# Counts for the first half of the nodes made during the deal; bucket rows stored by rounds

## The chip, the cores and the metric

The kernel runs on one core of one Trainium2 chip. The metric is device time in microseconds (us). The core has five engines that work side by side, each through its own list of instructions in order: TensorE (PE, matrix products into PSUM), VectorE (DVE), ScalarE (ACT), GpSimd (POOL, which here mostly issues indirect DMAs and a few additions), and SyncE (SP, which issues most of the other DMAs). They meet only through semaphores.

## The reference

The reference takes 3125 nodes with 256 features, 53,125 directed edges (`src`, `dst`) sorted by `dst`, and 16 attributes an edge. It runs four residual layers. The first is a message-passing layer over the edges, the third sums neighbours twice (SAGE), the second and fourth are mixtures without edges:

```python
x = x + gnn0(layernorm(x), edge_index, edge_attr)   # h = relu([x_src, x_dst, attr] @ mW1 + mb1); messages = h @ mW2 + mb2
                                                    # summed by src; then a two-layer update, residual
x = x + ffn0(layernorm(x))                          # shared MLP + 2 of 4 experts by a gate
x = x + gnn1(layernorm(x), edge_index)              # agg = segment_sum(x[src], tgt) / max(deg, 1); two such layers
x = x + ffn1(layernorm(x))                          # router keeps the top tokens, gelu MLP, scaled
```

For the third layer the kernel does not gather along edges. It multiplies by a **table of counts**, `adj_h`: for each pair of nodes, how many edges lead from the one to the other, as 16-bit floats. The table is in two halves, `half0` for targets below `H0` = 1152 and `half1` for the rest. Filling `half0` is what the change is about.

## The kernel before

**The deal** (`deal`). The edges stand in 416 columns of 128 edges, taken as 104 chunks of four columns. A *bucket* is a block of 32 source nodes; there are 98. For each chunk, `buckets` makes one-hots of the bucket numbers (VectorE), `select` turns them into ranks within the bucket by four products on PE, `place` (VectorE) works out the row of each edge in the DRAM buffer `cbuf`, and builds the record `rt` (68 floats, 272 bytes: a one-hot of the source within its bucket, the attributes in two halves, three fields on the target), and `put` sends the four columns with four indirect scatters from GpSimd (L438). `rt` has 20 buffers, so VectorE may run up to 20 chunks ahead of GpSimd. A bucket holds up to `ROUNDS` = 5 rounds of 128 edges by rank; since the edges come sorted by target, low ranks have low targets: round 0 has only targets below `H0`, round 1 both kinds, rounds 2 to 4 only the others. This is checked with the data at the end, and the result, `fits`, chooses between the branch described here and a general one.

Beside the dealing, three times a chunk (`piece`), a generator `tables` is advanced. It normalises the nodes and writes the first layer's products by node to `tab_a`, `tab_b`, `tab_h`, `own` over SP. At the start, unused places of `cbuf` are cleared over ScalarE's DMA queue. The order on PE, VectorE, ScalarE and SP is the order of the program, written out by hand; only GpSimd's is planned by the framework.

In `cbuf` the rows are laid out by group of four buckets: within a group, partition by partition, 20 rows of 272 bytes (5 rounds times 4 buckets) together.

**The edge stage** (`edges_by_bucket`). 25 groups of four buckets (the last has two, and is taken first), five rounds each: 125 steps. `begin` loads a group's rows (`rows<-cbuf`, L790) and its nodes' products (L795) over SP. A step runs: `fetch` gathers four times 128 rows of `tab_b` by target (POOL, L807), `turned` transposes (PE L826, copies `oT`), `spread` (PE L840, `pa`), the sum and the relu (DVE L845, ACT L850), `by_source` (PE L856). The loop places the next step's `spread` ahead of this step's `by_source`. Small parts of the layers that follow are put between (`pieces`), one pair of groups behind.

Between them also runs a generator `counts`, four advances a step, for the group before: `one_hots` makes for each round and bucket one-hots of the target (`oa`, 128 wide, L881; `ob`, 288 or 512 wide, L885), PE multiplies them (`pn`, L900), ScalarE copies the sum to 16 bits (`cn`, five buffers, L107), SP writes it to `adj_h` (L905, L909). A full group has per bucket a `half0` part (rounds 0 and 1, 288 wide) and a `half1` part (rounds 1 to 4, 512 wide):

```python
return (0,) * (r * P < BOTH1) + (1,) * (r * P >= BOTH0) if u["nb"] == 4 else (0, 1)   # halves(u, r)
for i, (hf, w) in enumerate(((half0, W0), (half1, W1))):                              # in counts(u)
```

`bank(...)` takes the next of a ring of PSUM banks, eight in the deal and three in the edge stage: an allocation waits until the third one before it has been read.

**The rest.** `sums_of_few` reads `adj_h` and does both neighbour sums (L1402), then the last layer. Neither is touched.

The change touches `deal` (clears, `ends`, `place`, `put`, the loop, the checks) and `edges_by_bucket` (`begin`, `halves`, `one_hots`, `counts`, and the index of a row in `rows`).

Of the kernel before, what the change touches and what calls it, by code (L numbers as in the profile page):

```python
# [8 lines left out]
F32 = mybir.dt.float32  # L9
# [7 lines left out]
P = 128  # L17
# [6 lines left out]
GB = 4  # L24
# [22 lines left out]
BOTH0, BOTH1 = P, 2 * P  # L47


@with_exitstack  # L50
def gnn_ffn_kernel(ctx: ExitStack, tc: tile.TileContext, a: dict, out: bass.AP):
# [130 lines left out]
    def deal():  # L182
# [11 lines left out]
        def clear(g, n):  # L194
            to = bass.AP(tensor=cbuf.tensor, offset=cbuf.offset + (g * P * PER + SURE * GB) * RW,
                         ap=[[PER * RW, P], [P * PER * RW, n], [1, (ROUNDS - SURE) * GB * RW]])
            nc.scalar.dma_start(to, empty.unsqueeze(1).to_broadcast([P, n, empty.shape[1]]))

        rest_of_last = bass.AP(tensor=cbuf.tensor, offset=cbuf.offset + full * P * PER * RW, ap=[[PER * RW, P], [1, SURE * GB * RW]])
        clear(full, 1)  # L200
        half_empty = (ROUNDS - SURE) * GB
        for o in range(0, SURE * GB, half_empty):
            n = min(half_empty, SURE * GB - o) * RW
            nc.scalar.dma_start(bass.AP(tensor=cbuf.tensor, offset=rest_of_last.offset + o * RW, ap=[[PER * RW, P], [1, n]]),
                                empty[:, :n])
        for g in range(0, full, 6):
            clear(g, min(6, full - g))
# [42 lines left out]
        nc.gpsimd.iota(past, pattern=[[P, ET]], base=GROUPS_OF * P * PER, channel_multiplier=1,  # L250
# [28 lines left out]
        def ends():  # L279
            nc.vector.tensor_copy(d_f, dst)  # L280
            nc.vector.scalar_tensor_tensor(base, b_i, float(CAP), past, op0=OP.mult, op1=OP.subtract)
            nc.vector.tensor_scalar(b_i, b_i, GB - 1, None, op0=OP.bitwise_and)
            nc.vector.scalar_tensor_tensor(base, b_i, float(1 - CAP), base, op0=OP.mult, op1=OP.add)
            nc.vector.tensor_scalar(b_i, src, BN - 1, None, op0=OP.bitwise_and)
            nc.vector.tensor_copy(scr, b_i)
            nc.vector.tensor_scalar(row[:, :, AT_SRC - BN], scr, 1.0, None, op0=OP.add)

            nc.vector.tensor_scalar(hi, d_f, float(W0), None, op0=OP.is_ge)
            for j in range(2, 8):
                at = float(W0 * j - (W0 - W1) * max(j - 4, 0))  # L290
                nc.vector.scalar_tensor_tensor(hi, d_f, at, hi, op0=OP.is_ge, op1=OP.add)
            nc.vector.scalar_tensor_tensor(scr, scr, 4.0, hi, op0=OP.mult, op1=OP.add)
            nc.vector.tensor_scalar(over, d_f, float(H0), float(P - 4), op0=OP.is_ge, op1=OP.mult)
            nc.vector.scalar_tensor_tensor(row[:, :, AT_SRC + 1 - BN], over, 1.0, scr, op0=OP.add, op1=OP.add)
            nc.vector.tensor_scalar(over, hi, -4.0, 0.0, op0=OP.add, op1=OP.max)
            nc.vector.scalar_tensor_tensor(over, over, float(W0 - W1), d_f, op0=OP.mult, op1=OP.add)
            nc.vector.scalar_tensor_tensor(over, hi, -float(W0), over, op0=OP.mult, op1=OP.add)
            nc.vector.tensor_scalar(row[:, :, AT_SRC + 2 - BN], over, 1.0, None, op0=OP.add)

        bad = pl.tile([P, 4], F32, name="bad")  # L300
# [80 lines left out]
        with tc.tile_pool(name="deal", bufs=3) as dp:  # L381
# [29 lines left out]
            def place(c, out):  # L411
# [11 lines left out]
                nc.vector.scalar_tensor_tensor(f, rnd, float(GB - P * PER), base[:, at], op0=OP.mult, op1=OP.add)  # L423
                nc.vector.scalar_tensor_tensor(f, rank, float(PER), f, op0=OP.mult, op1=OP.add)
                nc.vector.scalar_tensor_tensor(f, rank, float(CAP), f, op0=OP.is_lt, op1=OP.mult)
                nc.vector.tensor_tensor(to, f, past[:, at], op=OP.add)
                pos[c] = to
                rt = dp.tile([P, GB, RW], F32, name="rt", bufs=20)
# [5 lines left out]
            def put(c):  # L434
                rt, to = rts.pop(c), pos.pop(c)
                for i in range(GB):
                    n = min(P, E - (c * GB + i) * P)
                    one_of = nc.gpsimd.indirect_dma_start(  # L438
                        out=cbuf[:], out_offset=bass.IndirectOffsetOnAxis(ap=to[:n, i:i + 1], axis=0),
                        in_=rt[:n, i, :], in_offset=None)  # L440
                    tc.declare_no_dep(one_of.ins, group="deal", reason="no two have one place")
                    tc.add_to_no_dep_group("deal", one_of.ins)

            making = tables()
            totals[-1] = dp.tile([1, NBK], F16, name="none", bufs=1)
# [3 lines left out]
            def piece(c):  # L449
                if c > 0:  # L450
                    next(making, None)

# [50 lines left out]
            nc.vector.scalar_tensor_tensor(wrong, wrong, 1.0, whole, op0=OP.mult, op1=OP.mult, accum_out=bad[:, 2:3])  # L503
            rest = dp.tile([P, 1], F32, name="rest", bufs=1)
# [3 lines left out]
            nc.vector.tensor_scalar(fits, pf[:1, :1], 0.5, None, op0=OP.is_lt)  # L508

# [6 lines left out]
    def rest_of(fast):  # L516
# [259 lines left out]
        def edges_by_bucket():  # L776
            with tc.tile_pool(name="bk", bufs=2) as bp, tc.tile_pool(name="upd", bufs=2) as up, \
# [8 lines left out]
                def begin(g):  # L786
# [3 lines left out]
                    nc.sync.dma_start(rows.bitcast(F32).rearrange("p r w -> p (r w)"),  # L790
                                      cbuf[g * P * PER:(g + 1) * P * PER, :].rearrange("(p r) w -> p (r w)", p=P))
# [4 lines left out]
                    return dict(g=g, nb=nb, m=nb * BN, ag=ag, rows=rows, oa={}, ob={})  # L796

# [4 lines left out]
                def fetch(u, r):  # L802

                    cb = bp.tile([P, 4, HID], F32, name="cb", bufs=4)
                    for j in range(u["nb"]):
                        i = GB * r + j
# [4 lines left out]
                def halves(u, r):  # L811

                    return (0,) * (r * P < BOTH1) + (1,) * (r * P >= BOTH0) if u["nb"] == 4 else (0, 1)
# [7 lines left out]
                def turned(u, r):  # L821
# [3 lines left out]
                    for j in range(nb):  # L825
                        nc.tensor.matmul(pt[:2 * BN, j * P:(j + 1) * P], lhsT=u["rows"][:, GB * r + j, :2 * BN], rhs=ident_r,  # L826
# [25 lines left out]
                def by_source(u, r, hs):  # L852
                    if r == 0:
                        u["ph"] = pH.tile([P, HID], F32, name="ph")
                    for j in range(u["nb"]):
                        nc.tensor.matmul(u["ph"][j * BN:(j + 1) * BN, :], lhsT=u["rows"][:, GB * r + j, :BN].bitcast(F32),  # L856
# [16 lines left out]
                def one_hots(u, j, rs):  # L873


                    for r in rs:
                        field = u["rows"][:, GB * r + j, AT_SRC + 1:AT_SRC + 3].bitcast(F32)
# [4 lines left out]
                        w = W0 if halves(u, r) == (0,) else W1  # L882
                        ob = bp.tile([P, W1], F16, name="ob", bufs=12)
                        u["ob"][j, r] = ob
                        nc.vector.tensor_scalar(ob[:, :w], ids[:, 1:w + 1], field[:, 1:2], None, op0=OP.is_equal)  # L885

                def counts(u):
                    made, cut = None, ROUNDS // 2
                    for part in (range(cut), range(cut, ROUNDS)):
                        one_hots(u, 0, part)  # L890
                        yield
                    for j in range(u["nb"]):
                        for i, (hf, w) in enumerate(((half0, W0), (half1, W1))):
                            if j + 1 < u["nb"]:
                                one_hots(u, j + 1, range(cut, ROUNDS) if i else range(cut))
                                yield
                            pn = bank("pn")
                            rs = [r for r in range(ROUNDS) if (j, r, i) in u["oa"]]
# [8 lines left out]
                            made = hf[b * BN:(b + 1) * BN, :].rearrange("s (h l) -> (s h) l", l=w), cn[:, :w]  # L907
                            yield
# [599 lines left out]
```

## Time and profile before

| | us |
|---|---|
| time, median of 3 runs | 2128.87 (2125.72 to 2130.82) |
| the profiled execution's own time | 2130.54 |
| its span in the trace | 2128.7 |

| stretch of the span (us) | PE busy | DVE busy | ACT busy | POOL busy | clock of PE | DMA share |
|---|---|---|---|---|---|---|
| 0 to 33, loads and first chunks | 9.4 | 26.5 | 6.2 | 2.7 | 1.00 | 0.87 |
| 33 to 500, deal | 292.4 | 391.5 | 114.1 | 349.3 | 0.74 | 0.34 |
| 500 to 581, deal, last scatters | 0.2 | 0.9 | 0.0 | 61.4 | 0.50 | 0.08 |
| 581 to 625, edge stage starts | 20.0 | 15.7 | 16.8 | 22.5 | 0.66 | 1.02 |
| 625 to 1514, edge stage | 784.6 | 669.1 | 596.6 | 500.4 | 0.95 | 0.70 |
| 1514 to 1942, neighbour sums | 400.7 | 261.7 | 153.8 | 29.0 | 0.96 | 0.45 |
| 1942 to 2129, last layer | 177.1 | 113.3 | 50.9 | 19.0 | 0.98 | 0.05 |

How to read it. A row of a group of instructions gives line, engine, operation, `out<-in` by the program's names, shapes, the count, the busy time and the mean of one in ns, and behind the second bar the idle time before them with what ended it. Busy times of PE overlap, since products are pipelined; the distance from start to start says more. A line with `[1.03 <-DVE xn L127]` says that the engine had stood idle for 1.03 us until VectorE's instruction of line 127 let it go. "Landing" of a DMA is the time from its issue to its last data.

### The profile page before, as it was taken

The page shows a single profiled execution, that of the slowest core. Times are in us where ns is not written, and L with a number is a line of the kernel's source. Part 1 is how long each engine was busy: PE and PEld are TensorE (multiplying, and loading weights), DVE is VectorE, ACT ScalarE, POOL GpSimd, SP SyncE. Part 2 cuts the span into 40 slices and gives each one's busy share as a digit, 9 for nine tenths or more (in the row PEclk, how much of TensorE's full clock was granted, in tenths as well). Part 3 has the DMA queues.
Part 4 walks back from the last instruction along what each step waited for, and adds up shares of the span by engine and source line. Part 5 has one row for each costly group of instructions (what it writes and reads, how often), then busy time and mean ns, then how long its engine had stood idle before and what let it go on. Part 6 is the DMA issues. An engine that isn't in the chain of part 4 may idle for free. (4 is left out here: it accounts for less than half of the span.)

```text
span 2128.7 us, 25119 instructions
## 1 busy us (share of the span) xinstructions
PE 1684.2 (79%) x7419; PEld 1025.3 (48%) x7419; DVE 1478.7 (69%) x4078; ACT 938.4 (44%) x1695; POOL 984.3 (46%) x1044
## 2 busy tenths in 40 slices
PE   3667676661068898898889889888859999999998
PEld 1333232320034554455455546555537777886666
DVE  6888888883048877786777777677436675667960
ACT  1222222220046776676666666667333333443222
POOL 3677777777657655655565565555000000111011
PEclk9777777775579999999999999999979999999999
DMA  9432332320199776777667667774234545550010
GB/s 297 113 107 97 106 115 87 126 97 31 41 302 279 211 226 207 212 207 218 201 208 216 202 202 215 209 220 129 73 114 125 135 116 145 140 152 1 1 40 23
DMA packets 238441, 316.46 MB, mean 149 GB/s; under 512 B 34458, under 2 KB 168968, under 8 KB 237928
## 3 DMA queue, kind: packets, MB, share of 16 engines
q1 hardware_dynamic: 182216, 164.43, 25.6%
q0 software_dynamic: 52512, 142.96, 23.0%
q10 hardware_dynamic: 3568, 7.38, 1.0%
q8 instruction: 61, 1.00, 0.2%
q14 instruction: 84, 0.69, 0.1%
HBM read 229.71 MB, written 84.96 MB: 148 GB/s over the span
## 5 line engine op out<-in xcount | busy, mean ns | idle before, releaser
L807 POOL DMA_INDIRECT cb<-tab_b,goes_to x490 | 473.4, 966 | 372.4 <-issue 108.6
L438 POOL DMA_INDIRECT cbuf<-rt,to x416 | 410.4, 986 | 166.6 <-issue 98.6
L845 DVE TENSOR_TENSOR cb<-pa,cb 128x1024 f32<-128x1024 f32 x245 | 288.8, 1218 | 97.8 <-PE pa L840 57.4
L1402 PE MATMUL padj<-z,slab 128*128 128x512 f32 x1250 | 323.0, 411 | 15.3 <-DVE z L1311 15.3
L850 ACT ACTIVATE cb<-cb 128x1024 f32<-128x1024 f32 x245 | 254.9, 1051 | 58.0 <-DVE cb L845 57.1
L1402 PEld LDWEIGHTS padj<-z,slab 128*128 128x128 f32 x1250 | 233.6, 192 | 75.0 <-issue 23.0
L107 ACT ACTIVATE oT<-pt 64x512 fp32r<-64x512 f32 (+1 forms) x250 | 144.9, 580 | 176.7 <-PE pt L826 173.7
L900 PE MATMUL pn<-ob,oa 128*128 128x512 f16 (+1 forms) x596 | 153.4, 368 | 50.9 <-ACT cn L107 36.2
L130 POOL TENSOR_TENSOR x<-x,xn 128x256 f32<-128x256 f32 x25 | 24.6, 983 | 354.9 <-DVE xn L127 354.9
L840 PE MATMUL pa<-gives,oT 128*128 128x512 f32 x490 | 165.8, 460 | 22.7 <-ACT oT L107 10.4
L885 DVE TENSOR_SCALAR ob<-ids,rows 128x512 f16<-128x512 f16 (+1 forms) x490 | 171.9, 351 | 0.0
L881 DVE TENSOR_SCALAR oa<-ids,rows 128x128 f16<-128x128 f16 x596 | 150.3, 268 | 0.0
L343 PE MATMUL pp<-mw,xTa 128*128 128x512 f32 x200 | 137.7, 843 | 10.3 <-ACT xTa L107 10.3
L107 ACT ACTIVATE cn<-pn 128x288 f16<-128x288 f32 x196 | 97.2, 496 | 103.9 <-PE pn L900 90.4
L856 PE MATMUL ph<-cb,rows 128*32 128x512 f32 x980 | 140.9, 617 | 1.3 <-ACT cb L850 1.1
L900 PEld LDWEIGHTS <-oa 128*128 128x128 f16 x596 | 53.3, 100 | 162.9 <-issue 98.7
L331 PE MATMUL pt<-ident,xn 128*128 128x128 f32 x50 | 16.7, 438 | 134.8 <-DVE xn L326 134.8
L840 PEld LDWEIGHTS pa<-gives,oT 128*128 128x128 f32 x490 | 93.9, 204 | 54.3 <-ACT oT L107 15.0
L826 PE MATMUL pt<-ident_r,rows 128*64 128x128 f32 x490 | 52.8, 232 | 84.8 <-DMA rows<-cbuf 84.8
L1329 ACT ACTIVATE slab<-two 128x2048 fp32r<-128x2048 f16 x50 | 95.6, 1912 | 40.2 <-PE padj L1402 39.6
L107 ACT ACTIVATE total<-pk 1x98 f16<-1x98 f32 x103 | 24.5, 238 | 178.4 <-PE pk L404 178.3
L826 PEld LDWEIGHTS pt<-ident_r,rows 128*64 128x64 f32 x490 | 50.6, 143 | 106.3 <-issue 87.7
(242 smaller groups left out, 3040.0 us busy)
## 6 DMA issues: line engine op xcount, KB each, us to landing
two<-adj_h SPq DMA_DIRECT2D x24, 1600.0 KB, 7.7
rows<-cbuf SPq DMA_DIRECT2D x25, 680.0 KB, 9.2
adj_h<-cn SPq DMA_DIRECT2D x100, 128.0 KB, 3.1
gives<-tab_h SPq DMA_DIRECT2D x48, 256.0 KB, 10.8
cb<-tab_b,goes_to POOLq DMA_INDIRECT x490, 4.4
adj_h<-cn SPq DMA_DIRECT2D x100, 72.0 KB, 3.3
cbuf<-rt,to POOLq DMA_INDIRECT x416, 2.2
cbuf<-empty ACTq DMA_DIRECT2D x4, 1632.0 KB
```

Of the source, the lines that this page charges most:

```text
L107: nc.scalar.activation(dst, src, AF.Copy)
L343: nc.tensor.matmul(pp, lhsT=xT[:, c, :], rhs=mw1[:, 2 * h + c, :], start=c == 0, stop=c == 1)
L438: one_of = nc.gpsimd.indirect_dma_start(out=cbuf[:], out_offset=bass.IndirectOffsetOnAxis(ap=to[:n, i:i + 1], axis=0), in_=rt[:n, i, :], i ...
L807: nc.gpsimd.indirect_dma_start(out=cb[:, j, :], out_offset=None, in_=tab_b[:], in_offset=bass.IndirectOffsetOnAxis(ap=u["to"][:, i:i + 1], ...
L840: nc.tensor.matmul(got[j // 2][:, j % 2, :], lhsT=oT[:, j, :], rhs=u["ag"][:, j, :], start=True, stop=True)
L845: nc.vector.tensor_tensor(cb[:, j:j + 2], pa, cb[:, j:j + 2], op=OP.add)
L850: nc.scalar.activation(h, h, AF.Relu)
L856: nc.tensor.matmul(u["ph"][j * BN:(j + 1) * BN, :], lhsT=u["rows"][:, GB * r + j, :BN].bitcast(F32), rhs=hs[j // 2][:, j % 2, :], start=r ...
L881: nc.vector.tensor_scalar(oa, ids[:, 1 + i * P:1 + (i + 1) * P], field[:, 0:1], None, op0=OP.is_equal)
L885: nc.vector.tensor_scalar(ob[:, :w], ids[:, 1:w + 1], field[:, 1:2], None, op0=OP.is_equal)
L900: nc.tensor.matmul(pn[:, :w], lhsT=u["oa"].pop((j, r, i)), rhs=u["ob"][j, r][:, :w], start=r == rs[0], stop=r == rs[-1])
L1402: nc.tensor.matmul(pa, lhsT=slab[:, c, :], rhs=(z2 if second else z1)[:, c, :], start=c == 0, stop=c == NB - 1)
```

## The change

Rows in `cbuf` are laid out by rounds: all groups' rows of one round stand together, the rounds in falling order, the spare rows (for edges that have no place) first. `STRIDE` is one round of all groups. Scatters from chunk `LATE` = 70 on are declared to reach only the part `cbuf[:PLACED]`, which leaves out rounds 0 and 1 of the full groups, and edges that would go beyond it are sent to the spare rows, which two more checks report.

A new generator, `early_counts`, makes the `half0` parts of the 96 buckets of full groups: it reads rounds 1 and 0 back from `cbuf` (three groups at a time, over SP), makes their one-hots, products and copies, and writes `adj_h`. It is advanced three times a chunk from chunk 90 on, and what is left of it is run at the end of `deal`. The edge stage makes only the `half1` parts of full groups; the last, small group is as before. `rt` has 19 buffers in place of 20. The rows of a group are loaded in five pieces a partition.

```diff
+STRIDE = GROUPS_OF * P * GB
+LATE = 70
+PLACED = ET * P + (ROUNDS - BOTH1 // P) * STRIDE + P * GB
...
-        clear(full, 1)
...
-        for g in range(0, full, 6):
-            clear(g, min(6, full - g))
+        def places(g, at, n):
+            return bass.AP(tensor=cbuf.tensor, offset=cbuf.offset + (ET * P + at * STRIDE + (g + 1) % GROUPS_OF * P * GB) * RW,
+                           ap=[[GB * RW, P], [STRIDE * RW, n], [1, GB * RW]])
+        nc.scalar.dma_start(places(full, ROUNDS - SURE, SURE),
+                            empty[:, :GB * RW].unsqueeze(1).to_broadcast([P, SURE, GB * RW]))
+        per = (ROUNDS - SURE) * STRIDE // P
+        some, times = empty.shape[1] // RW, 5
+        for o in range(0, per, some * times):
+            to = bass.AP(tensor=cbuf.tensor, offset=cbuf.offset + (ET * P + o) * RW,
+                         ap=[[per * RW, P], [some * RW, times], [1, some * RW]])
+            nc.scalar.dma_start(to, empty.unsqueeze(1).to_broadcast([P, times, some * RW]))
...
+                if c >= LATE:
+                    sum_of = dp.tile([P, GB], F32, name="sum_of")
+                    nc.vector.tensor_tensor(sum_of, f, past[:, at], op=OP.add)
+                    nc.vector.scalar_tensor_tensor(f, sum_of, float(PLACED), f, op0=OP.is_lt, op1=OP.mult)
                 nc.vector.tensor_tensor(to, f, past[:, at], op=OP.add)
                 pos[c] = to
-                rt = dp.tile([P, GB, RW], F32, name="rt", bufs=20)
+                rt = dp.tile([P, GB, RW], F32, name="rt", bufs=19)
...
-                        out=cbuf[:], out_offset=bass.IndirectOffsetOnAxis(ap=to[:n, i:i + 1], axis=0),
+                        out=cbuf[:] if c < LATE else cbuf[:PLACED], out_offset=bass.IndirectOffsetOnAxis(ap=to[:n, i:i + 1], axis=0),
...
+            def early_counts():
+                rows, oas, obs, made = {}, {}, {}, None
+                n = BOTH1 // P
+                half0 = adj_h[:H0 // P * NP, :].rearrange("(s b) c -> s (b c)", b=H0 // P)
+                def fetch(g):
+                    t = tmp.tile([P, pieces[1] * P], F32, name="ea", bufs=2)
+                    m = n * GB * RW
+                    for i in range(min(3, full - g)):
+                        v = t[:, i * m:(i + 1) * m].rearrange("p (r w) -> p r w", r=n)
+                        nc.sync.dma_start(v, places(g + i, ROUNDS - n, n))
+                        rows[g + i] = v.rearrange("p r (j w) -> p r j w", j=GB)
+                def one_hots(b):
+                    if b % (3 * GB) == GB and b // GB + 2 < full:
+                        fetch(b // GB + 2)
+                    both = tmp.tile([P, ET], F32, name=("scr", "hi", "over")[b % 3]).bitcast(F16)
+                    for r in range(n):
+                        v = both[:, r * (P + W0):(r + 1) * (P + W0)]
+                        field = rows[b // GB][:, r, b % GB, AT_SRC + 1:AT_SRC + 3]
+                        oas[b, r], obs[b, r] = v[:, :P], v[:, P:]
+                        nc.vector.tensor_scalar(oas[b, r], ids[:, 1:1 + P], field[:, 0:1], None, op0=OP.is_equal)
+                        nc.vector.tensor_scalar(obs[b, r], ids[:, 1:1 + W0], field[:, 1:2], None, op0=OP.is_equal)
+                fetch(0)
+                yield
+                one_hots(0)
+                for b in range(full * GB):
+                    if b + 1 < full * GB:
+                        one_hots(b + 1)
+                    yield
+                    pn = bank("pn")
+                    for r in range(n):
+                        nc.tensor.matmul(pn[:, :W0], lhsT=oas.pop((b, r)), rhs=obs.pop((b, r)), start=r == 0, stop=r == n - 1)
+                    cn = dp.tile([P, W0], F16, name="cn", bufs=2)
+                    copy(cn, pn[:, :W0])
+                    if made:
+                        nc.sync.dma_start(*made)
+                    made = half0[b * BN:(b + 1) * BN, :].rearrange("s (h l) -> (s h) l", l=W0), cn
+                    yield
+                nc.sync.dma_start(*made)
...
             def piece(c):
                 if c > 0:
                     next(making, None)
+                if c >= LATE + 20:
+                    next(counting, None)
...
+            at = LATE * GB
+            nc.vector.scalar_tensor_tensor(whole[:, at:], ranks[:, at:], float(BOTH1), whole[:, at:], op0=OP.is_lt, op1=OP.mult,
+                                           accum_out=bad[:, 3:4])
+            nc.vector.tensor_scalar(low[:, at:], src[:, at:], float(NBK * BN), None, op0=OP.is_lt)
+            nc.vector.scalar_tensor_tensor(low[:, at:], ranks[:, at:], float(P), low[:, at:], op0=OP.is_lt, op1=OP.mult,
+                                           accum_out=bad[:, 4:5])
...
+            for _ in counting:
+                pass
...
-                    nc.sync.dma_start(rows.bitcast(F32).rearrange("p r w -> p (r w)"),
-                                      cbuf[g * P * PER:(g + 1) * P * PER, :].rearrange("(p r) w -> p (r w)", p=P))
+                    src = bass.AP(tensor=cbuf.tensor, offset=cbuf.offset + (ET * P + (g + 1) % GROUPS_OF * P * GB) * RW,
+                                  ap=[[GB * RW, P], [STRIDE * RW, ROUNDS], [1, GB * RW]])
+                    nc.sync.dma_start(rows.bitcast(F32).rearrange("p (r j) w -> p r (j w)", r=ROUNDS), src)
...
-                    return (0,) * (r * P < BOTH1) + (1,) * (r * P >= BOTH0) if u["nb"] == 4 else (0, 1)
+                    return (1,) * (r * P >= BOTH0) if u["nb"] == 4 else (0, 1)
...
                 def counts(u):
-                    made, cut = None, ROUNDS // 2
-                    for part in (range(cut), range(cut, ROUNDS)):
+                    made, rs = None, [r for r in range(ROUNDS) if halves(u, r)]
+                    parts = rs[:2], rs[2:]
+                    for part in parts:
                         one_hots(u, 0, part)
                         yield
                     for j in range(u["nb"]):
-                        for i, (hf, w) in enumerate(((half0, W0), (half1, W1))):
+                        for i, (hf, w) in list(enumerate(((half0, W0), (half1, W1))))[u["nb"] == 4:]:
                             if j + 1 < u["nb"]:
-                                one_hots(u, j + 1, range(cut, ROUNDS) if i else range(cut))
+                                one_hots(u, j + 1, parts[i])
                                 yield
...
+                        if u["nb"] == 4 and j + 1 < u["nb"]:
+                            one_hots(u, j + 1, parts[0])
+                            yield
                             yield
```

## The prediction

> **What bounds the kernel now.** I read the time slices first, then windows around the end of the deal, then what TensorE waits for in the edge stage.
>
> Two of the slice rows (40 slices of 53.2 us, busy tenths):
>
> ```profile
> DVE  6888888883048877786777777677436675667960
> POOL 3677777777657655655565565555000000111011
> ```
>
> VectorE drops to 3 and then 0 in slices 10 and 11 while GpSimd goes on. The windows of 20 us there (columns: PE, weight loads, VectorE, ScalarE, GpSimd busy; clock; DMA share; GB/s):
>
> ```profile
> 480.00:500.00 20.00, 4.44 (x12) 1.21 (x11) 18.40 (x66) 2.06 (x9) 15.44 (x15) 0.50 0.08 27
> 500.00:520.00 20.00, 0.19 (x2) 0.11 (x2) 0.91 (x5) 0.00 (x0) 15.19 (x16) 0.50 0.08 26
> 560.00:580.00 20.00, 0.00 (x0) 0.00 (x0) 0.00 (x0) 0.00 (x0) 15.12 (x17) 0.50 0.09 28
> 580.00:600.00 20.00, 1.85 (x6) 1.23 (x6) 2.65 (x7) 1.01 (x3) 7.59 (x10) 0.50 0.90 221
> ```
>
> So GpSimd's scatters end the deal: one per 1.264 us (0.96 busy, 0.30 idle), the last done at 580.2, stage two opening at 581.4. VectorE ended its last check at 501.3. For **80 us** PE, VectorE, ScalarE and SyncE do nothing.
>
> From 625 to 1514 us the edge stage has PE busy 785 of 889 us, VectorE 669, ScalarE 597, GpSimd 500. PE is nearest to the bound; what it waits for from 635 to 1500 (total us, times, longest):
>
> ```profile
> PE pn L900 <- ACT cn L107: 36.2, 20, 2.2
> PE pagg L607 <- ACT hT L107: 25.7, 11, 2.4
> PE pd L578 <- ACT cn L107: 8.4, 13, 1.9
> ```
>
> The counting itself causes 44.6 us of some 104 us idle. One such place on PE's timeline:
>
> ```profile
> 955.90 1.04 PE L900 MATMUL pn<-ob,oa 128*128 128x512 f16 x4
> 957.97 0.73 PE L138 MATMUL pt<-ident,xn 128*128 128x128 f32 x4 [1.03 <-DVE xn L127]
> 960.91 0.64 PE L900 MATMUL pn<-ob,oa 128*128 128x288 f16 x2 [2.21 <-ACT cn L107]
> 962.13 1.86 PE L900 MATMUL pn<-ob,oa 128*128 128x512 f16 x4 [0.58 <-ACT xT L107]
> 963.43 2.27 PE L840 MATMUL pa<-gives,oT 128*128 128x512 f32 x4
> ```
>
> The bank ring has three banks. The 288-wide `pn` needs the bank of the 512-wide `pn` three allocations earlier, whose copy sits on ScalarE behind a relu that waits for VectorE. What follows is slow: four 512-wide products take 1.86 us instead of 1.04, `pa` 2.27 instead of 1.18.
>
> **The change, part by part.** The groups that are moved:
>
> ```profile
> L881 DVE TENSOR_SCALAR oa<-ids,rows 128x128 f16<-128x128 f16 x596 | 150.3, 268 | 0.0
> L885 DVE TENSOR_SCALAR ob<-ids,rows 128x288 f16<-128x288 f16 x96 | 29.7, 309 | 0.0
> L900 PE MATMUL pn<-ob,oa 128*128 128x288 f16 x202 | 44.0, 295 | 40.8 <-ACT cn L107 36.2 <-DVE ob L885 4.4
> L107 ACT ACTIVATE cn<-pn 128x288 f16<-128x288 f32 x98 | 39.6, 404 | 71.7 <-PE pn L900 71.6
> adj_h<-cn SPq DMA_DIRECT2D x100, 72.0 KB, 3.3
> ```
>
> *Removed from stage two*, for each of 96 buckets: two `oa`, one 288-wide `ob`, two 288-wide products, one copy of 0.40 us, one 72 KB DMA. `ob` of the second round stays, for the upper half. On the timeline instructions overlap, so I use start-to-start: `oa` 0.16, `ob` 0.20, hence 0.52 us of VectorE a bucket (50 us in all); on PE 0.24 us a bucket (the 512-wide ones are 0.217 apart, times 288/512, twice), 23 us in all; its bounds are the 0.15 and 0.41 us that the timeline shows for a pair. VectorE and ScalarE are not the bound, so their 50 and 39 us count only through PE's waits. The remaining `pn` goes to the place of the 288-wide one (last in a step), so its bank is wanted three allocations after quick copies, not after the late one. I take half of the 44.6 us, 22, since PE then meets `xn` and `hT` sooner. The cold stretch after 960.91 costs, start to start and against the same four products elsewhere in the pair of groups, 1.30-0.87 (`pn`), 2.07-1.08 (`pa`) and 2.28-1.32 (`pz`) = 2.4 us; such a place comes once in each of 12 pairs, 29 us; I take a third, 10. The last drain (1496.5 to 1506 us) has half its `pn` gone: 3. Sum **-58 us**; ends: 14+3 = -17 (no wait goes) and 39+45+29 = -113.
>
> Here a rule is weighed: "TensorE: Matmul & The Clock Gate", Part 1, lets the clock fall to half only after an idle window of about 3.4 us. No wait here is over 2.4 us, so by the rule the 10 us are nothing (-48). But the window with this place has clock 0.85 (950 to 985 us), the one before 1.00; I keep the row.
>
> *Added to the deal, in the loop.* Two small VectorE operations for chunks 70 to 103: 68 times 0.20 (0.163 and a gap) = 13.6 us. The generator is advanced in chunks 90 to 103, three times each, 42 times: that finishes 20 buckets and makes one-hots of 22, each 2 x (0.16+0.20) = 0.72 us: 16 us. First rows awaited: 3. VectorE idles 17% from 440 to 480 us, which absorbs about 7. So placing ends at 523 instead of 496.6; the checks (4.8 us before, 1.2 more for three operations on 136 columns) end at 529. GpSimd then has 11 chunks of 5.06 us ahead of it, so it is not starved: its end is unmoved. PE gets 20 x 0.5 us in the loop, where it is 60 to 70% busy. The first fetch on SP needs the scatters of chunks under 70, issued by 580.2-34x4x1.264 = 408 us; SP gets there at about 445, so table writes queued behind it are not held.
>
> *Added at the deal's end.* 76 buckets remain and are drained with no other work. VectorE would need 74 x 0.72 = 53 us, ending at 582, inside the cover. But **`cn` has two buffers here** (five in stage two): copy b needs DMA b-2 landed. Two buckets cost copy 0.40 + handing over 0.05 + landing + waking ScalarE 0.1. Landings in the trace for this tile:
>
> ```profile
> DMA to landing us min/median/max: 1.6/3.2/8.2
> ```
>
> 1.6 stands in the last drain, where the DMA share is 0.27; 3.3 is the median of the 72 KB form under a share of 0.70. The deal's end has 0.09 of scatters, plus this stream (128 packets of 63 ns, by the SP queue's 15,972 packets in 21.1% of 16 engines' time from 900 to 1200 us, over 16 engines: 0.5 us a bucket) and the row fetches. I take 1.8: 2.35/2 = 1.17 us a bucket, 89 us, plus some 1 us for each of five row fetches (0.8 MB in front of a `cn`) = 94. End 529+94 = 623, against 581: **+42 us**. Ends: +8 (VectorE sets the pace; 53 us and the last product, copy and issue) and +98 (landing 3.3: 1.93 x 76 = 146, and 5). SP issues 96 more DMAs here (0.32 us each) and 24 fetches; it is not full.
>
> A second rule speaks against the change: "SBUF — State Buffer", Who interferes with whom, says that a VectorE `tensor_scalar` in a two-port mode locks GpSimd out for the whole instruction. The one-hots would then slow the scatters, up to their 62% duty: 40 scatters x 0.8 = +31 us, POOL ending at 612. In stage two, thick with the same one-hots, POOL's gathers take 966 ns against 958 ns for quiet scatters, so I take 0; either end lies before 623.
>
> *Layout.* Scatters are as many and as long; the clears write the same 7.4 MB. Row loads keep 680 KB but in pieces of 1088 B instead of 5440 B. They land in 9.2 us and are first read some 13 us after issue (898.9 to 912.1), so 4 us of slack hide it: 0; past that, up to 24 x 2 = 48 us.
>
> **Sum:** 2130.5 (the profiled execution's own time, span 2128.7) +42-58 = 2114.5; that execution lies 1.7 us above the median, 2128.87, so 2113 in its terms.
>
> **Rivals.** *B, the drain is hidden* (VectorE's pace, +8 to +15) and the waits go (-65): about 2075. For it: the 80 us hole, landings of 1.6. Against: two buffers. 0.15. *C, the `cn` ring takes the place of the hole, slower:* landings as in stage two, +98-58 = +40: 2169. It decides from where the drain reaches 581+58 = 639: (110-5)/76 = 1.38 us a bucket, a landing of 2.2 us. For it: 2.0 to 2.6 us for `tab_b` and `tab_h` writes in the deal. Against: those are 256 KB, several in a row. 0.24. *D, stage two gives its stream alone*, 17 to 25 us, as the waits move to `hT`, `xn` or row loads: +42-20: 2151, slower. For it: ScalarE and VectorE are long chains in half the windows. 0.18. *E, the early fetch waits for every scatter issued before it* (chunk 89 ends at 509 us), or the flag falls (35840/98 = 366 edges a bucket by chunk 70, 256 needed): later by 25 us and more: 0.03. My case, A: 0.40.
>
> **How the numbers follow.** 0.2%, 4.3 us, is about what can be told from no change. A is faster in nine of ten of its spread, B always; C, D and E are slower nearly always: faster 0.53, same 0.05, slower 0.42. For 8 in 10 the range takes in most of B and C: 2062 to 2168. A's own is 2090 to 2136.
>
> **What would show it.** The hole after 500 us filled; scatters still ending near 580; stage two opening near 623; in the drain ScalarE's copies 1.2 us apart, waiting for `adj_h` DMAs; no 288-wide `pn` after it but the last group's; PE's waits for `cn` under 25 us; the edge stage 58 us shorter. I am wrong if copies stand under 0.9 or over 1.4 us apart, or the edge stage shrinks by less than 35 us.

## The result, and the profile after

The changed kernel takes **2144.12 us** (median of 5 runs, 2143.14 to 2151.94) against 2128.87: a ratio of 1.008, interval 1.006 to 1.010. It is slower by 15 us where 2113 was forecast. The profiled execution has a span of 2142.3 us and a mean TensorE clock of 0.887, as before.

VectorE's slice row of the changed kernel (40 slices of 53.6 us, busy tenths):

```profile
DVE  6888888889735778677767776777427766667960
```

The empty stretch is gone: VectorE has 7 and 3 in slices 10 and 11. The windows by stage, of the kernel before and then of the changed one (columns: PE, weight loads, VectorE, ScalarE, GpSimd busy, with counts; clock; DMA share; GB/s):

```profile
501.00:581.00 80.00, 0.17 (x2) 0.06 (x2) 0.15 (x1) 0.00 (x0) 60.54 (x64) 0.50 0.09 27
581.00:1514.00 933.00, 804.56 (x4192) 473.11 (x4193) 684.76 (x1928) 613.45 (x1037) 522.86 (x558) 0.94 0.71 212
1514.00:2128.00 614.00, 577.78 (x2300) 414.14 (x2298) 374.93 (x767) 204.69 (x283) 48.01 (x57) 0.96 0.33 89
```

```profile
534.00:632.00 98.00, 45.82 (x154) 18.98 (x154) 58.41 (x298) 30.52 (x76) 39.14 (x40) 0.50 0.38 114
632.00:1529.00 897.00, 769.19 (x4000) 456.21 (x4001) 634.74 (x1640) 588.90 (x940) 516.81 (x558) 0.95 0.73 213
1529.00:2142.00 613.00, 575.96 (x2301) 412.32 (x2299) 374.43 (x767) 204.45 (x283) 48.07 (x57) 0.97 0.33 89
```

VectorE's checks now end at 534.3 us, not 501.3. GpSimd's last scatter ends at 584.4, not 580.2. But the 76 buckets that are still uncounted at 534 hold the deal until 630, and the edge stage opens at 631.8 instead of 581.4: **+50 us**. From there to the first load of `two` (the neighbour sums' first read of `adj_h`) it takes 897.7 us instead of 933.0: **-35 us**. What follows is 1.5 us shorter. +50-35-1.5 is the difference of the two profiled executions, 13.6 us; between the medians it is 15.

Two things decide this: the drain (the counting that is left when the dealing has ended) is the long thing after 534 us, about as forecast, and the edge stage gave back only 35.

**The drain.** ScalarE's waits from 534 to 632 us (total us, times, longest), and SyncE's timeline within it (start, length of the run of issues, engine, line, what, count; `ea` is the tile into which `early_counts` reads rows back):

```profile
ACT cn L113 <- DMA adj_h<-cn: 61.4, 45, 4.5
```

```profile
573.07 1.41 SPq L469 DMA_DIRECT2D ea<-cbuf  x3
574.58 13.62 SPq L496 DMA_DIRECT2D adj_h<-cn  x12
588.29 1.41 SPq L469 DMA_DIRECT2D ea<-cbuf  x3
```

ScalarE waits for its own buffer to land, 61 of 98 us. Twelve buckets and one fetch of rows take 588.29-573.07 = 15.2 us. Between fetches the copies come in pairs, one pair every 2.12 us, so 1.06 us a bucket and 12.7 us for twelve. The other 2.5 us come with the fetch: its 0.8 MB are issued on SP's queue ahead of a `cn`, which then lands in 3.6 to 4.6 us where most others take 1.6.

**The edge stage.** In the two windows PE is busy 804.6 and 769.2 us, so it is idle 128.4 and 127.8. The 35 us are busy time, and the waiting is as long in sum as it was. By groups of products, the 288-wide `pn` had 44.0 us of busy time (the row of the kernel before stands in the prediction) and now has 2.4, for the last group:

```profile
L971 PE MATMUL pn<-ob,oa 128*128 128x288 f16 x10 | 2.4, 284 | 1.2 <-DVE ob L956 1.2
```

All other products of the stage together took as long as before: the busy times of their groups add up to within 1 us of what they were (the 512-wide `pn` 111.4 and now 116.0, `pa` 165.8 and 169.7, others as much less). Where products overlap they share time, so that 41.6 us less of the one group are 35 less of PE's. What PE waits for, one line of the kernel before (582 to 1515 us), then the changed kernel from 632 to 1530 us (total, times, longest):

```profile
PE pn L900 <- DVE ob L885: 6.8, 11, 2.2
```

```profile
PE pn L971 <- DVE ob L956: 52.9, 33, 2.7
PE pagg L675 <- ACT hT L113: 26.5, 12, 2.4
PE pn L971 <- DVE aT L679: 12.4, 11, 2.1
PE pd L646 <- ACT cn L113: 0.4, 1, 0.4
```

The 44.6 us of waits for copied counts are gone to 0.4. In their place stand 52.9 us for one-hots, where there were 6.8. One place, PE's timeline of the changed kernel, and two lines of VectorE's:

```profile
1068.88 1.23 PE L971 MATMUL pn<-ob,oa 128*128 128x512 f16 x4 [1.77 <-DVE ob L956]
1076.36 1.89 PE L971 MATMUL pn<-ob,oa 128*128 128x512 f16 x4 [2.40 <-DVE ob L956]
1077.69 2.01 PE L912 MATMUL pa<-gives,oT 128*128 128x512 f32 x4
```

```profile
1073.33 2.33 DVE L917 TENSOR_TENSOR cb<-pa,cb 128x1024 f32<-128x1024 f32 x2
1075.96 0.34 DVE L956 TENSOR_SCALAR ob<-ids,rows 128x512 f16<-128x512 f16 x1
```

`counts` is advanced four times a step. In the new order the first advance makes half of a bucket's one-hots, the second nothing, the third the other half of the bucket after it, and the fourth has the product of the first bucket. So the product reads one-hots that were made in its own step. On VectorE those stand behind the two additions `cb` (L917, together 2.3 us) and behind `xn`, and PE reaches the product up to 2.7 us before they are done.

### The profile page after: what moved, and what is told of

The parts are those of the page before. It is cut to its first block, busy times and chain, and to the rows that moved or that the text cites. A ratio compares the mean times of both kernels' runs of the same rounds, so it can differ in the third digit from the quotient of the medians.

```text
span 2142.3 us, 25407 instructions
## 1 busy us (share of the span) xinstructions
PE 1707.9 (80%) x7419; PEld 1031.0 (48%) x7419; DVE 1524.9 (71%) x4249; ACT 950.7 (44%) x1695; POOL 983.3 (46%) x1044
## 4 chain that ended last, share of the span: by engine, by line
PE 52%; DVE 23%; DMA 12%; issue 5%; ACT 5%; POOL 2%; SPq 1%; DVEq 0%; another core or an unknown queue 0%; ACTq 0%; POOLq 0%
PE padj L1477 13%; PE pd L646 6%; DMA cb<-tab_b,goes_to 5%; PE pp L352 4%; PE py L1525 4%; DVE cb L917 4%; DMA adj_h<-cn 3%; PE pn L971 3%; PE pa L912 3%; PE ph L928 3%; PE pz L1307 2%; PE pd L686 2%; ACT cb L922 2%; DVE ranks L427 2%; PE pz L810 2%
## 5 line engine op out<-in xcount | busy, mean ns | idle before, releaser
L879 POOL DMA_INDIRECT cb<-tab_b,goes_to x490 | 467.6, 954 | 392.5 <-issue 109.6
L451 POOL DMA_INDIRECT cbuf<-rt,to x416 | 415.4, 998 | 165.8 <-issue 97.9
L917 DVE TENSOR_TENSOR cb<-pa,cb 128x1024 f32<-128x1024 f32 x245 | 288.7, 1217 | 108.9 <-PE pa L912 76.5
L922 ACT ACTIVATE cb<-cb 128x1024 f32<-128x1024 f32 x245 | 250.3, 1051 | 43.6 <-DVE cb L917 41.2
L113 ACT ACTIVATE cn<-pn 128x288 f16<-128x288 f32 (+1 forms) x196 | 97.3, 500 | 220.3 <-PE pn L971 111.8
L912 PE MATMUL pa<-gives,oT 128*128 128x512 f32 x490 | 169.7, 468 | 18.8 <-ACT oT L113 8.7
L971 PE MATMUL pn<-ob,oa 128*128 128x512 f16 (+1 forms) x404 | 118.2, 409 | 66.1 <-DVE ob L956 52.9
L956 DVE TENSOR_SCALAR ob<-ids,rows 128x512 f16<-128x512 f16 x394 | 141.4, 359 | 0.0
L953 DVE TENSOR_SCALAR oa<-ids,rows 128x128 f16<-128x128 f16 x404 | 108.7, 272 | 0.0
L971 PEld LDWEIGHTS <-oa 128*128 128x128 f16 x404 | 40.1, 102 | 122.4 <-DVE ob L956 58.8
L1529 POOL TENSOR_TENSOR y<-y,fb 128x256 f32<-128x256 f32 x25 | 18.3, 732 | 159.3 <-ACT y L1528 159.3
L352 PEld LDWEIGHTS pp<-mw,xTa 128*128 128x128 f32 x200 | 53.3, 286 | 73.5 <-issue 56.4
## 6 DMA issues: line engine op xcount, KB each, us to landing
cbuf<-empty ACTq DMA_DIRECT2D x5, 1360.0 KB, 16.6
```

What stands on the lines that cost most here:

```text
L113: nc.scalar.activation(dst, src, AF.Copy)
L352: nc.tensor.matmul(pp, lhsT=xT[:, c, :], rhs=mw1[:, 2 * h + c, :], start=c == 0, stop=c == 1)
L451: one_of = nc.gpsimd.indirect_dma_start(out=cbuf[:] if c < LATE else cbuf[:PLACED], out_offset=bass.IndirectOffsetOnAxis(ap=to[:n, i:i + 1 ...
L879: nc.gpsimd.indirect_dma_start(out=cb[:, j, :], out_offset=None, in_=tab_b[:], in_offset=bass.IndirectOffsetOnAxis(ap=u["to"][:, i:i + 1], ...
L912: nc.tensor.matmul(got[j // 2][:, j % 2, :], lhsT=oT[:, j, :], rhs=u["ag"][:, j, :], start=True, stop=True)
L917: nc.vector.tensor_tensor(cb[:, j:j + 2], pa, cb[:, j:j + 2], op=OP.add)
```

## The experiments

*Theory 1*: the drain is set by two `cn` buffers. *Theory 2*: the edge stage's missing gain is the place of the one-hots. The rivals: the drain is set by VectorE, by PE at half clock or by SP's queue, or rows stored by rounds cost something; and the gain is missing because PE is held by other chains anyway.

All runs of this section were made later, on four chips on which every kernel, the one before too, takes some 7% longer than in the first measurement. On which chip that one was made is not on record; "the first chip" means it, whichever it was. Each run is compared with the kernel before on its own chip (2279 to 2291 us), and stages are compared among these runs alone. The times in us that the first expectations give were meant for the first chip's pace. A further kernel, without early counts and with the first half of the table unfilled, gave no time; the edge stage's part alone is taken from a difference below.

### The changed kernel again, and the layout alone

> The changed kernel once more, beside the runs that follow, since the chip of the first four runs took 7% longer for every kernel. On a chip like that of the first measurement: 1.008 of the kernel before. On one like that of the four runs: e1's and e3's distances put it at 1.02 to 1.03.

> The kernel before with the rows of buckets stored by rounds (clears, scatter places, five-piece row loads), all counts in the edge stage as before and no early ones. Theory: the layout costs nothing, ratio 0.998 to 1.002. Rival, the row loads' smaller pieces hold up the edge stage: 10 us or more slower.

The second keeps the rows by rounds in memory, without early counts, with nothing sent to spare rows early, and with the edge stage's counts in the old order:

```diff
-LATE = 70
+LATE = 1000
...
-                if c >= LATE + 20:
-                    next(counting, None)
...
-                    return (1,) * (r * P >= BOTH0) if u["nb"] == 4 else (0, 1)
+                    return (0,) * (r * P < BOTH1) + (1,) * (r * P >= BOTH0) if u["nb"] == 4 else (0, 1)
...
```

The changed kernel takes 2333.16 us, 1.025 [1.0212, 1.0287] of the kernel before there. The layout alone takes 0.9992 [0.9976, 1.0007]: it **costs nothing** that can be told from no change, and with it the row loads in five pieces.

The changed kernel lost 15 us on the first chip and 51 here. The layout-only kernel shows what is missing. Its windows from the end of the checks on:

```profile
646.00:660.00 14.00, 0.01 (x1) 0.00 (x0) 0.15 (x1) 0.00 (x0) 10.12 (x12) 0.50 0.08 25
660.00:1680.00 1020.00, 843.53 (x4194) 491.72 (x4195) 685.71 (x1929) 618.51 (x1037) 523.35 (x558) 0.90 0.67 194
```

Here the empty stretch that the counts were to fill is 14 us long, not 80. The scatters are as short (958 ns in the median) but the dealing loop is slower: from 100 to 600 us VectorE has 62 to 67 us of work in each 100 us where it has 85 to 87 on the first chip, and much of the idle time of PE's weight loads and GpSimd there is put down to `issue`, up to 10 us at once. What stalls them the profile doesn't say, and no run tried it. In the changed kernel on these chips the scatters end with the loop, near 650, and nothing covers the drain.

### The deal's cost alone

> The changed kernel with the early counts, but the edge stage makes all counts as before (the first half of the table is written twice, with the same values). It leaves the cost of the deal alone. Theory: stage two opens 50 us later than before and takes as long as before, so 50 us over the kernel before and some 35 over the changed one. Rival, the edge stage's gain of 35 us came from somewhere else than the counts taken out of it: less than 20 over the changed one.

The changed kernel with the full, old counts put back in the edge stage, so that `half0` of the full groups is written twice with the same numbers:

```diff
-                    return (1,) * (r * P >= BOTH0) if u["nb"] == 4 else (0, 1)
+                    return (0,) * (r * P < BOTH1) + (1,) * (r * P >= BOTH0) if u["nb"] == 4 else (0, 1)
...
```

2381.86 us, 1.044 [1.0410, 1.0469]. Its edge stage opens at 752.1 us (layout alone: 660.0) and takes 1016.7 us (1019.7). So the deal's part of the change costs 92 us here by the profiles and the edge stage doesn't feel it; by the medians it is 2381.86-2279.06 = 103 (the profiled execution of the layout alone was 15 us above its median). The changed kernel opens at 747.9 and takes 968.6: the edge stage's part gives 48 to 51 us, 49 by the medians. 50 and 35 had been expected: without its cover the deal's part costs twice that, and the edge stage's part gives more than on the first chip. The theory holds against its rival: the gain comes from the counts that were taken out.

### Five count buffers in the deal

> The changed kernel with five `cn` buffers in the early counts (and 17 `rt` buffers to make room). Theory 1, the ring of two buffers sets the drain's pace: copies come some 0.75 us apart (VectorE's 0.72), the drain ends near 595 instead of 630, stage two opens near 597, time about 2110. Rival, the DMAs themselves (bandwidth or issue) or PE at half clock set the pace: copies stay over 1.0 us apart, time over 2138.

```diff
-                rt = dp.tile([P, GB, RW], F32, name="rt", bufs=19)
+                rt = dp.tile([P, GB, RW], F32, name="rt", bufs=17)
...
-                    cn = dp.tile([P, W0], F16, name="cn", bufs=2)
+                    cn = dp.tile([P, W0], F16, name="cn", bufs=5)
```

2305.02 us, 1.0124 [1.0088, 1.0160] where the changed kernel has 1.025. The edge stage opens at 712.1 us instead of 749.8, 38 sooner where 35 were expected. The drain's window of the changed kernel (its later repetition) and of this one:

```profile
653.00:750.00 97.00, 44.79 (x151) 18.33 (x149) 57.05 (x296) 30.70 (x76) 0.42 (x1) 0.50 0.34 102
```

```profile
654.00:712.00 58.00, 55.34 (x154) 16.00 (x154) 54.95 (x300) 28.99 (x76) 1.07 (x2) 0.50 0.57 171
```

The same 76 copies take 58 us instead of 97, 0.76 a bucket, and now VectorE is busy 55 of the 58. Theory 1 holds. The next limit is VectorE's one-hots, 0.72 us a bucket: the weight loads of the products wait for them, 34 us in all. PE at half clock did not set the pace with two buffers: the clock is 0.50 in both windows. SP's queue is not the limit: in the kernel with both edits, below, twelve buckets and a fetch pass it in 687.30-677.96 = 9.3 us (15.2 with two buffers), so the deeper ring covers most of the fetch too.

```profile
677.96 1.41 SPq L469 DMA_DIRECT2D ea<-cbuf  x3
679.47 7.73 SPq L496 DMA_DIRECT2D adj_h<-cn  x12
687.30 1.41 SPq L469 DMA_DIRECT2D ea<-cbuf  x3
```

### One-hots one step earlier

> The changed kernel with a bucket's one-hots of the edge stage made one step earlier, so that no `pn` needs one-hots of its own step. Theory 2, PE's new waits for `ob` (52.9 us) are a matter of order: they fall under 10 us, the edge stage is 20 to 40 us shorter, time about 2115. Rival, VectorE's or another engine's own work limits those steps: PE waits as long for something else, time over 2138.

```diff
...
+                    early = u["nb"] == 4
+                    if early:
+                        one_hots(u, 1, rs)
+                        yield
...
-                        if u["nb"] == 4 and j + 1 < u["nb"]:
-                            one_hots(u, j + 1, parts[0])
+                        if early and j + 1 < u["nb"]:
+                            if j + 2 < u["nb"]:
+                                one_hots(u, j + 2, parts[0])
                             yield
                             yield
+                            if j + 2 < u["nb"]:
+                                one_hots(u, j + 2, parts[1])
+                                yield
```

2313.00 us, 1.0147 [1.0116, 1.0177]. Windows of the edge stage, changed kernel (its later repetition) and this one:

```profile
750.00:1716.00 966.00, 794.59 (x4001) 468.19 (x4001) 637.53 (x1641) 589.83 (x941) 516.13 (x558) 0.92 0.68 197
```

```profile
751.00:1700.00 949.00, 796.63 (x4000) 464.55 (x4001) 636.64 (x1640) 588.14 (x940) 520.29 (x558) 0.92 0.69 201
```

PE does the same work in 17 us less, a little under the 20 to 40 expected: idle 152 us instead of 171. Theory 2 holds for the greater part. In the changed kernel there, `pn` waiting for `ob` is the largest of PE's waits (31.6 us, 20 times); in this one it is 2.5 us, 3 times. Against the layout alone the edge stage is now 70 us shorter (1019.7 to 949.7), with PE's idle time down by 24. The rest of the idle time stays, and PE meets other waits in it:

```profile
PE pn L975 <- DVE aT L679: 18.9, 10, 2.7
PE pagg L675 <- ACT hT L113: 19.8, 6, 5.4
```

so the rival holds for a remainder. How much of the wait turns into time varies. Six profiles with this order, counting those of the kernels below, have edge stages of 943 to 965 us and PE idle for 152 to 170 of them; three without it have 966 to 971 and 170 to 176. In all six the product's wait for `ob` is under 3 us; but the longest of the six has 60 us of waits put down to `issue`, the others 27 to 43 (those without the order 37 to 65).

### Both

> Five `cn` buffers and one-hots a step ahead together. If both theories hold the gains add: about 2083, under the kernel before (2129). If the two shortened stretches hide each other's gain, 2100 or more.

> Five `cn` buffers and one-hots a step ahead, again. Theory: 45 to 65 us below the changed kernel beside it (drain 30 to 40, edge stage 20 to 25), whatever the chip. On a chip like the first one that is under the kernel before, ratio about 0.98. If only the slow chip gave those gains, under 30 us.

> The changed kernel once more, as the mate of the two that follow on the same chip. Two outcomes are foreseen. On a chip whose VectorE gets through the dealing loop by 535 us, as on the chip of the first profile: 1.006 to 1.010 of the kernel before, next stage opened at 632 us. On a chip whose loop ends only near 650 us, as on the two chips of the other runs: 1.021 to 1.029, next stage opened near 748 us, because the scatters then end with the loop and no empty 80 us are left to count in.

> Five count buffers in the deal and the one-hots one step earlier in the edge stage, once more. If the two costs found are those of the first chip too, then on a chip whose loop ends by 535 us the drain of 76 buckets takes 57 us in place of 96 (next stage opened at 593 us), the edge stage is 20 us shorter than the changed kernel's, and the kernel takes 0.970 to 0.985 of the one before. On a chip whose loop ends near 650 us: 0.996 to 1.001, as twice before. If the order of the one-hots cost nothing on the first chip, 0.988 there.

The two edits together took 0.9986 [0.9969, 1.0004], 0.9983 [0.9965, 1.0000] and 0.9987 [0.9968, 1.0006] on three chips, beside 1.0250 and 1.0258 [1.0222, 1.0293] for the changed kernel on two of them. The gains add: 2333.16-2276.33 = 57 us, where the one alone gives about 28 and the other about 24 (1.025 less 1.0124 and less 1.0147, of 2280 us). Where the drain is uncovered this just pays for the change: the three intervals end at or close to 1. On the first chip, where the loop ends at 534 us, a drain of 57 us would open the edge stage at some 593 and the order would give about 20 more: an estimate of 2144-39-20 = 2085 us, 0.98, from the drains and the order's gain measured here. No run shows it, since on no later chip did the loop end so soon.

### Counts begun sooner, and two at a time

> The kernel of the line above, with the early counts begun 16 chunks sooner (from chunk 74 in place of 90). Theory 1, a bucket that is counted inside the dealing loop is free where VectorE is busy for 65 of 100 us of it and a bucket that is left for the drain costs 0.75 us: 24 buckets move from the drain into the loop, the next stage opens 18 us sooner (694 us in place of 712), 0.990 to 0.993 of the kernel before on a chip whose loop ends near 650 us. Theory 2, what VectorE does is added to the loop's length whatever its busy share, since the loop's chunks wait for each other across engines: the loop ends about 18 us later, the drain is as much shorter, and the time is that of the line above within 0.3%. On a chip whose VectorE is busy for 87 of 100 us in the loop, both expect no gain.

```diff
-                if c >= LATE + 20:
+                if c >= LATE + 4:
                     next(counting, None)
```

2265.73 us, **0.9919 [0.9897, 0.9940]**: a version that beats both kernels, by under 1% and shown on one chip. Windows of the loop's last part and of what follows the checks, for this kernel:

```profile
480.00:656.00 176.00, 92.19 (x310) 41.82 (x308) 148.62 (x585) 42.47 (x136) 112.59 (x115) 0.67 0.33 107
657.00:696.00 39.00, 37.09 (x103) 10.64 (x101) 36.64 (x199) 20.15 (x52) 0.41 (x1) 0.50 0.55 164
```

The loop ends where it did (656.6 us, against 655.5 in the third run of both edits), with VectorE at 149 of 176 us instead of 135, and the drain is 39 us instead of 57. A bucket in the loop is free while VectorE has room, and costs 0.75 us in the drain: theory 1 of that run, 18 us expected, 16.6 measured at the stage's opening (712.9 to 696.3).

> The early counts begun at chunk 74 and, at each of the three places of a chunk, two steps of them in place of one: about 90 of the 96 buckets are made inside the dealing loop. Theory 1, a bucket inside the loop costs the loop nothing until VectorE is full: VectorE needs 0.70 us a bucket over some 170 us of loop, so its busy time goes from 75 (without counts: 65) to about 100 of 100 us; the loop ends up to 12 us later (656 to 668), the drain is under 6 us, and the next stage opens at 664 to 676 us in place of 696: 0.980 to 0.987 of the kernel before. Theory 2, a step that is put between a chunk's own is paid by the chunk once the free share is small: the loop ends 30 us or more later, and the time is 0.990 or more.

Against the kernel just shown:

```diff
                 if c >= LATE + 4:
                     next(counting, None)
+                    next(counting, None)
```

2272.58 us, 0.9922 [0.9895, 0.9949] on another chip: no further gain.

```profile
480.00:684.00 204.00, 126.62 (x408) 52.47 (x408) 186.67 (x782) 61.10 (x185) 121.53 (x118) 0.66 0.39 122
684.00:691.00 7.00, 4.54 (x16) 1.68 (x16) 3.86 (x21) 2.89 (x7) 0.41 (x1) 0.50 0.24 75
```

The drain is down to 7 us, but the loop ends 28 us later, at 684, with VectorE at 187 of 204 us. Between 84% and 92% of VectorE's time the free room seems to end. That the dealing chunks, whose work passes between four engines, then meet a busy VectorE is an explanation, not a measurement: the chip is another one, the kernel before takes 9 us longer on it, and how much of the 28 us is the chip's is not shown. The second theory is near to this step (30 us or more later, 0.990 or more), the first was right about the one before.

## Why the prediction was wrong

*The hole at the deal's end* was read rightly. Scatters end the deal before, at 580; VectorE's work was forecast to end at 529 and did at 534.3; GpSimd's end moved by 4 us.

*The drain* was the best step: 94 us forecast, 96 measured. That it came so close is in part luck: inside it two terms were off and cancelled. A bucket took 1.06 instead of 1.17 us (landing 1.6, not 1.8), and a fetch of rows 2.5 instead of 1. The stage opened 50 us later where the sum said 42: 5 us of the difference are the checks, 2 the drain, and 1.4 the time from the last count to the opening. The "two buffers" argument was then confirmed by the five-buffer run.

*The shared port*: a scatter beside an idle VectorE before, and one beside VectorE's one-hots after:

```profile
537.73 0.96 POOL L438 DMA_INDIRECT cbuf<-rt,to  x1 [0.31 <-DMA cbuf<-rt,to]
```

```profile
537.50 1.17 POOL L451 DMA_INDIRECT cbuf<-rt,to  x1 [0.30 <-issue]
```

From 536 to 546 us, where VectorE is busy with one-hots all the time, the scatters take 1.17 us and start 1.47 apart, not 0.96 and 1.26. Where VectorE pauses they are as before. So 0 was a little too low: the scatters after 534 lost some 2 us together. The prediction's comparison, 966 against 958 ns, was a mean over a whole stage, in which this drowns. The rule of the Trainium skill ("SBUF — State Buffer", Who interferes with whom) would have slowed them by up to 31 us; less than a tenth of that was measured. Neither mattered, since the last scatter ended at 584.4 and the drain at 630.

*Layout*: forecast 0, measured 0.9992 [0.9976, 1.0007]; in the changed kernel a row load lands in 9.7 instead of 9.2 us.

*The edge stage* is **the step that failed**: -58 forecast, -35 measured. The sentence "I take half of the 44.6 us, 22, since PE then meets `xn` and `hT` sooner" has no counterpart: PE's idle time went from 128.4 to 127.8. The waits for `cn` went whole, 44.6 to 0.4, and those for `ob` rose from 6.8 to 52.9 us. I had argued only where the remaining product would sit in the PSUM ring, from the allocations. I had not followed what the new order asks of VectorE: that half of a bucket's one-hots is made in the same step as the product that reads it, behind two additions of 1.2 us. The run with the one-hots a step earlier shows that this order costs time: 19 us of idle time go. That was on another chip, where the wait for `ob` was 31.6 us and not 52.9; how much of the 22 us an earlier order would give on the first chip is not shown.

Of the other terms, 23 us of PE's stream, 10 of slow clock and 3 of the last drain are together 36, and 35 came, but this agreement is luck. The busy time that went is that of the removed products, so the stream was worth some 35 us, near the upper of the two bounds of 14 and 39. The slow places are still there, as at 1076 us, and the other products took no less time: the 10 us came to nothing.

*The rivals.* D, "stage two gives its stream alone, as the waits move", was nearest (2151, edge stage -20): its mechanism, waits that move, is what happened, though to the one-hots and not to `hT`, `xn` or row loads. It had 0.18. The sign of being wrong, "the edge stage shrinks by less than 35 us", was missed by less than half a microsecond. The time lies in the range (2062 to 2168), outside A's own (2090 to 2136); the direction was wrong. The balance of +42-58 turns to +6 once the term of 22 is gone, and the later opening, +50 for +42, makes it +14.

*The clock rule* of the Trainium skill ("TensorE: Matmul & The Clock Gate", Part 1, an idle window of about 3.4 us): the row was kept, and as to the clock the row was right. In the changed kernel the granted clock is 1.00 before the wait of 2.40 us, 0.50 from 1076 to 1079 and 1.00 again from 1080; the four products after the wait took 1.89 us. After the wait of 1.77 us it stayed at 1.00 and they took 1.23. In the kernel before it is 0.50 from 960 to 966, after the wait of 2.21 us. So in this trace waits shorter than the page's figure cost clock, and the measurement decides. What the forecast had wrong is that such places would cost less after the change.

## What to carry to other kernels

Work that is moved into an empty stretch is free only as far as the stretch reaches at the pace of its narrowest ring: before moving it, work out the round trip of one buffer (copy, landing, wake) over the number of buffers, times the count, and if that is longer than the stretch, start sooner, in a stage whose busiest engine still has room. When an instruction is taken out of a hand-written order, list for what remains who must have produced its operands and in which slot of the same step they are now made; a wait that is removed tells nothing of the one that stood just behind it. A gain that rests on a stretch of idle time can be lost elsewhere: in a later run the same stage left 14 us of it instead of 80.

## What the runs showed of the hardware

On four chips the same programs ran 7% slower than in the first measurement. The loss is in stages where many engines hand work to each other: the deal's loop ends at 646 instead of 501 us (layout alone against the kernel before), and the edge stage with all its counts takes 1020 instead of 933, with PE busy 39 us longer at a granted clock of 0.90 instead of 0.94 and idle 48 us longer; the neighbour sums and the last layer take 612 against 614. In the loop the trace marks much of the lost time as `issue`. Its cause stays open.

A small write issued behind a large read on the same queue landed late: a 72 KB `cn` landed in 1.6 us in the drain, and in 3.6 to 4.6 behind the 0.8 MB of a row fetch. Whether it waits in the queue or shares the DMA engines with the read was not separated.

f16 one-hots without a pause on VectorE stretched GpSimd's indirect scatters beside them from 0.96 to 1.17 us each.

The granted clock of PE fell from 1.00 to 0.50 within waits of 2.2 and 2.4 us in an otherwise busy stage and came back some 3 to 6 us after PE had gone on; after a wait of 1.8 us it had not fallen.
